# A convolution block on one core: reordered seams between stages, and products that nothing reads

## The chip, the cores and the metric

The kernel runs on one core of one Trainium2 chip. Its measure is the device time of one execution in microseconds (us); where several executions are timed, their median counts. A separate execution was recorded by the hardware profiler. All operands are 32-bit floats.

## The reference

The input x has 16 images of 192 channels and 64 x 64 pixels. The first layer computes

```python
h = ln2d(x)                                    # over the channels of each pixel
projected, gate = split(conv1x1(h, 192 -> 384))
projected = dwconv3(projected, dw_k)
scanned = mix of four directional scans of projected (lr, rl, tb, bt)
mixed = (scanned + dwconv3(projected, le_k)) * sigmoid(gate)
mixed = gelu(batch_norm(mixed))                # mean and variance over all images and pixels
x = x + conv1x1(mixed, out_proj)
x = x + conv1x1(gelu(conv1x1(ln2d(x), fc1: 192 -> 768)), fc2: 768 -> 192)
```

The second layer averages every image over its pixels, passes the averages through two small matrices (192 to 48 to 192 x 9) and so gets a 3 x 3 filter for each channel of each image, of which a mask keeps four taps. It filters each image with its own taps and adds a bias.

## The kernel before

The work is in three stages, each with its own pools in SBUF. The order of instructions on every engine is written out by hand; nothing is planned by the framework. Images go in pairs, one on partitions 0 to 63 and one on 64 to 127; `HALF` names these two slices, and the 192 channels are three tiles of 64, indexed by `t`.

**First stage** (lines 246 to 584): 64 chunks of four pixel groups (`AR`). `load_a` (L466) fetches a chunk three chunks ahead, one image from SP and one from GpSimd. `turn` (L479) transposes a chunk on TensorE (L484) into the one PSUM tile `xt`, so that VectorE can take the statistics of each pixel (`variance`, L488: L491 and L492). `deviation` (L494) gets the reciprocal root with ScalarE (L496) and VectorE (L497). `project` (L500) multiplies the untransposed pixels with the projection weights (L512), two PSUM tiles for each image half, and evicts with the scale of each pixel, on VectorE (L517) and ScalarE (L518), into a staging tile: `stg` for even blocks of four chunks, `mid` for odd ones. `store` (L533) writes a block to DRAM during the next four chunks, on GpSimd and SP, so a staging tile has to be stored before the block after the next writes it. Ahead of the loop, `projection_weights` (L272) scales the weights on VectorE (L277), takes their column means on TensorE (L281) and subtracts them (L284). Small jobs hang on chunk numbers by `beside`: among them `load_dm` and `load_lm` (L186, L192), which fetch the second stage's filter matrices, half from SP and half from GpSimd.

**Second stage** (lines 587 to 789): 24 groups of eight channels, 96 steps. Vertical and local filters are products with banded matrices (L618, L662), horizontal scans run on VectorE (L653, L655), `gate` (L686) multiplies by the sigmoid and, at the end of a group, stores it to `mixed_d` in DRAM (L704). The statistics of the batch norm end with `spread` (L715) and `batch_norm` (L726). The last group lies in `mid`.

**Third stage** (lines 792 to 1096): 128 chunks of 512 pixel positions. `load_y` (L209) fetches two chunks of `mixed_d`, for the first eight chunks into `ximg[1]`, which is not used yet; `unmix` (L844) transposes them back on VectorE (L239), `bn_gelu` (L850) is on ScalarE (L852, L853), `out_proj` (L874: L880 for channels 128 to 191, L884 for 0 to 127) on TensorE, `residual` (L887) adds the input `x2` into the image tile `ximg` (L890) and forms the sums over channel tiles (L894, L905). `mean` (L907, L913) turns such sums into means; `center` (L915, L920) subtracts them, `squares` (L924) squares (L927) and sums again (L928, L905), `normalize` (L933) takes the root (L936), loads the Gelu table by a one-element activation (L938), and multiplies by the reciprocal (L939, L940). `first` (L942) is the product with fc1 (L952) and its GELU (L954), `second` (L957) that with fc2 (L825, called from `both`), `final` (L966) adds it to the image (L972). The loop at L1057 interleaves one step of each of several chunks, from -3 on:

```python
    for n in range(-3, n_ch + 1):
        at(load, n + 3)
        at(unmix, early_)
        at(first, n, 0)
        at(bn_gelu, early_)
        products(n, 0)
```

`products(n, t)` (L855) puts a mean of chunk n + 1 and the output product of chunk n + 2 into one PSUM tile of two banks, tag `f1`, of which there are two and which `first` uses too. Tag `f2` has three banks, tag `a` one. When a pair's last chunk is final, `pooled`, `squeeze` (L988) and `excite` (its products again are L825, tile `ps_k`) give the taps.

**The tail** (lines 1098 to 1118) filters the last pair in 12 pieces of 16 rows (four row groups by three channel tiles): five on ScalarE (L1026) and VectorE (L65), seven as products with taps on diagonals (L1103, L1035) evicted by ScalarE (L1037). All use an output tile `ol` of tag `gl`, of which there are four. The pieces are stored from SP, GpSimd and ScalarE (L1041, L1044).

## Time and profile before

| | |
|---|---|
| median of 3 runs | 3750.83 us (3748.33 to 3751.44) |
| profiled execution, its own time | 3738.29 us |
| its span, first to last instruction | 3736.5 us |
| TensorE busy | 3686.8 us, 99% of the span |
| VectorE busy | 2706.0 us, 72% |
| ScalarE busy | 1786.6 us, 48% |
| GpSimd busy | 420.2 us, 11% |
| mean granted clock of TensorE | 0.994 |

In the profile PE is TensorE's matrix product, PEld its weight load, DVE VectorE, ACT ScalarE, POOL GpSimd and SP the engine that only issues transfers; POOLq, ACTq and SPq are their queues. A line such as "L952 PE MATMUL ps_f<-h,wf" gives the line of the kernel, the engine, the operation, and the tile written and read. A 32-bit product appears as two records, a transpose as one. "Granted clock" is the share of TensorE's full clock that it was allowed. Times in the timeline count from the start of the span. The first stage takes the time up to about 636 us, the second to about 1310, the third the rest, the tail its last 40.

### The profile page before, as it was taken

The page shows a single profiled execution, that of the slowest core. Times are in us where ns is not written, and L with a number is a line of the kernel's source. Part 1 is how long each engine was busy: PE and PEld are TensorE (multiplying, and loading weights), DVE is VectorE, ACT ScalarE, POOL GpSimd, SP SyncE. Part 2 cuts the span into 40 slices and gives each one's busy share as a digit, 9 for nine tenths or more (in the row PEclk, how much of TensorE's full clock was granted, in tenths as well). Part 3 has the DMA queues.
Part 4 walks back from the last instruction along what each step waited for, and adds up shares of the span by engine and source line. Part 5 has one row for each costly group of instructions (what it writes and reads, how often), then busy time and mean ns, then how long its engine had stood idle before and what let it go on. Part 6 is the DMA issues. An engine that isn't in the chain of part 4 may idle for free.

```text
span 3736.5 us, 71017 instructions
## 1 busy us (share of the span) xinstructions
PE 3686.8 (99%) x30252; PEld 1649.4 (44%) x30252; DVE 2706.0 (72%) x4164; ACT 1786.6 (48%) x1945; POOL 420.2 (11%) x683
## 2 busy tenths in 40 slices
PE   8999999999999979999999999999999999999998
PEld 5666656555555533333333333333333333333333
DVE  6887776999999965557666766766766766675763
ACT  3434434888888833334334434434443443443432
POOL 2334332101011020000000000000000000000000
PEclk9999999999999989999999999999999999999999
DMA  6899997999999841112212222222222221221212
GB/s 163 241 252 243 265 280 238 308 294 283 280 283 271 226 100 27 51 44 63 78 56 66 69 67 62 69 61 68 74 57 58 76 71 42 80 75 43 69 37 74
DMA packets 308427, 491.74 MB, mean 132 GB/s; under 512 B 46656, under 2 KB 202640, under 8 KB 308112
## 3 DMA queue, kind: packets, MB, share of 16 engines
q1 hardware_dynamic: 250064, 295.14, 29.5%
q0 software_dynamic: 57152, 190.94, 18.7%
q8 instruction: 239, 3.92, 0.4%
q10 hardware_dynamic: 896, 1.12, 0.1%
q14 instruction: 76, 0.62, 0.1%
HBM read 284.91 MB, written 197.92 MB: 129 GB/s over the span
## 4 chain that ended last, share of the span: by engine, by line
PE 96%; DMA 2%; DVE 1%; SPq 0%; POOL 0%; issue 0%; ACT 0%; ACTq 0%; DVEq 0%; POOLq 0%
PE ps_f L952 27%; PE ps_f L825 27%; PE ps_pj L512 12%; PE ps_l L662 11%; PE ps_d L618 7%; PE ps_o L884 5%; PE ps_xt L484 2%; PE ps_o L880 2%; PE ps_o L913 1%; DMA xa<-in_x_dram 1%; PE ps_k L825 0%; DMA ximg<-mixed_d 0%; DMA mixed_d<-mid 0%; SPq L472 0%; PE ps_d L1035 0%
## 5 line engine op out<-in xcount | busy, mean ns | idle before, releaser
L954 ACT ACTIVATE gl<-ps_f,bf 128x1024 f32<-128x1024 f32 x384 | 427.6, 1114 | 1316.2 <-PE ps_f L952 1316.2
L952 PE MATMUL ps_f<-h,wf 64*64 64x512 f32 x9216 | 1035.8, 594 | 6.8 <-DVE h L940 6.7
L825 PE MATMUL ps_f<-gl,place 128*64 128x512 f32 x4608 | 1022.2, 592 | 0.0
L952 PEld LDWEIGHTS ps_f<-h,wf 64*64 64x64 f32 x9216 | 334.5, 133 | 693.8 <-issue 642.6
L825 PEld LDWEIGHTS ps_f<-gl,place 128*64 128x64 f32 x4608 | 334.2, 137 | 574.5 <-issue 533.4
L512 PE MATMUL ps_pj<-wi,xa 64*128 64x384 f32 x3072 | 515.6, 488 | 3.5 <-DVE stg L517 3.5
L920 DVE TENSOR_TENSOR h<-ximg,ps_o 128x768 f32<-128x768 f32 x128 | 116.4, 951 | 425.3 <-PE ps_o L884 417.0
L512 PEld LDWEIGHTS ps_pj<-wi,xa 64*128 64x128 f32 x3072 | 294.3, 187 | 196.8 <-issue 12.2
L890 DVE SCALAR_TENSOR_TENSOR ximg<-ps_o,pt,low 128x256 f32<-128x256 f32 x384 | 168.0, 479 | 266.8 <-PE ps_o L884 266.8
L65 DVE SCALAR_TENSOR_TENSOR o<-ximg,taps,o 128x1024 f32<-128x1024 f32 x252 | 323.2, 1282 | 9.1 <-ACT o L1011 2.6
L1015 POOL DMA_DIRECT2D out_dram<-o x168 | 87.9, 528 | 2067.6 <-DVE o L65 2064.8
L939 DVE RECIPROCAL rs<-rs 128x512 f32<-128x512 f32 x64 | 214.3, 3349 | 27.0 <-ACT rs L936 27.0
L653 DVE TENSOR_TENSOR_SCAN v<-tab,q 128x1024 f32<-128x1024 f32 x96 | 218.3, 2274 | 6.8 <-ACT tab L641 6.8
L655 DVE TENSOR_TENSOR_SCAN v<-tab,q 128x1024 f32<-128x1024 f32 x96 | 217.5, 2266 | 0.0
L518 ACT ACTIVATE stg<-ps_pj,rsa 128x384 f32<-128x384 f32 x128 | 120.5, 945 | 188.7 <-PE ps_pj L512 178.5
L884 PE MATMUL ps_o<-low,wo 128*64 128x256 f32 x1536 | 210.0, 395 | 0.0
L641 ACT ACTIVATE tab<-mask,dec_b 128x1024 f32<-128x1024 f32 x192 | 209.8, 1146 | 0.0
L518 ACT ACTIVATE mid<-ps_pj,rsa 128x384 f32<-128x384 f32 x128 | 120.8, 944 | 181.7 <-PE ps_pj L512 174.7
L491 DVE BATCH_NORM_STATS2 st<-ps_xt 128x6 f32<-128x192 f32 x512 | 173.8, 340 | 17.3 <-PE ps_xt L484 17.1
L239 DVE STREAM_TRANSPOSE low<-low 128x512 f32<-128x512 f32 x174 | 167.7, 1016 | 2.1 <-issue 0.3
L972 DVE SCALAR_TENSOR_TENSOR ximg<-ps_f,pt,ximg 128x512 f32<-128x512 f32 x192 | 134.4, 749 | 40.2 <-PE ps_f L825 37.8
L472 POOL DMA_DIRECT2D xa<-in_x_dram x192 | 119.8, 630 | 362.6 <-PE ps_pj L512 285.0
(197 smaller groups left out, 4060.1 us busy)
## 6 DMA issues: line engine op xcount, KB each, us to landing
low<-in_x_dram SPq DMA_DIRECT2D x128, 384.0 KB
out_dram<-o POOLq DMA_DIRECT2D x168, 256.0 KB, 3.7
mid<-pg_d SPq DMA_DIRECT2D x8, 4096.0 KB
low<-mixed_d SPq DMA_DIRECT2D x116, 256.0 KB
low<-pg_d SPq DMA_DIRECT2D x7, 4096.0 KB
pg_o<-pg_d SPq DMA_DIRECT2D x7, 4096.0 KB
xa<-in_x_dram POOLq DMA_DIRECT2D x192, 128.0 KB, 5.6
xa<-in_x_dram SPq DMA_DIRECT2D x192, 128.0 KB
```

Source lines behind the costliest of these rows:

```text
L65: nc.vector.scalar_tensor_tensor(o, in0, scalar, in1, ALU.mult, ALU.add, **kw)
L512: nc.tensor.matmul(ps[i], pixels(n, t, g)[q], wi[q, t].rearrange("p g k c -> p (g k c)"), start=(t == 0), stop=(t == 2))
L518: nc.scalar.activation(stag[blk][1][:, :, j], ps[1], AF.Copy, scale=rs[:, g, 1:2])
L618: nc.tensor.matmul(dst(ps[o, ih]), mats[g % 2]["dm"][q, di + 1, :, ch], src(s["pg"][q, :, 0, ch]), start=(di == 0), stop=stop)
L653: nc.vector.tensor_tensor_scan(vf, tab, q, 0.0, ALU.mult, ALU.add)
L655: nc.vector.tensor_tensor_scan(vf[:, ::-1], tab[:, ::-1], q[:, ::-1], 0.0, ALU.mult, ALU.add)
L662: nc.tensor.matmul(dst(bst[k]["ps"][o, i]), lm_of(g)[q, m, :, c], src(q, ih), start=start, stop=stop)
L825: nc.tensor.matmul(ps[q], w(i), rhs(i), start=start, stop=stop)
L884: nc.tensor.matmul(ps[q, wh].rearrange("p (r w) -> p r w", w=32), wo[:, 64 * t:64 * t + 64], cols(rows(s["mx"][:, i]))[:, :, wh], start=Fa ...
L939: nc.vector.reciprocal(rs, rs)
L952: nc.tensor.matmul(pf[o, i], wf1[q, t, m0:m0 + 64], s["h"][q, t], start=(t == 0), stop=(t == 2))
L954: nc.scalar.activation(gl, pf, AF.Gelu, bias=bf1[:, m:m + 1])
```

## The change

It has six parts.

1. Opening: `ones` is set first, and 24 products of `ones` with `ones` follow on TensorE, which nothing reads. The weights' means and their subtraction stand ahead of the first transposes. In chunk 0, the first two pixel groups are projected ahead of chunk 1's transposes, and chunk 1's statistics are taken beside the last two groups, two groups' worth beside each.
2. The four loads of filter matrices hang on chunks 46, 48, 50 and 52 instead of 46 to 49.
3. `mid` is the first tile of its pool, and `ximg[1]` is allocated ahead of `ximg[0]`, so `ximg[1]` and not `ximg[0]` lies where `mid` was.
4. The store of the last group is cut in two, half from SP and half from GpSimd.
5. The loop of the third stage starts at chunk 1. What came before is written out: chunk 0's output product takes the columns of channels 0 to 127 first, the means of chunk 0 come from products over all three channel tiles (`mean_part`) instead of from sums on VectorE, they lie in a bank of their own, the squares are taken in two halves, the Sqrt table is loaded early, and the output products of chunks 0 to 2 are placed between. `idle(k)` issues k products that nothing reads, of 128 x 128 weights and 512 columns: two before the output product of chunk 0, one ahead of `first(0, 0)`; in the last chunk two behind `pooled` and one behind `excite`.
6. The tail's five pieces on ScalarE and VectorE write to tiles of tags `o` and `h2`.

```diff
+    mid = ce.tile([128, SB_], F32, tag="mid", name="mid")
     ones = ce.tile([128, 128], F32, tag="ones", name="ones")
...
-        beside(46, load_dm, 0)
-        beside(47, load_lm, 0)
-        beside(48, load_dm, 1)
-        beside(49, load_lm, 1)
+        for i in range(2):
+            beside(46 + 4 * i, load_dm, i)
+            beside(48 + 4 * i, load_lm, i)
...
-        def project(n):
+        def project(n, groups, beside_it):
...
-            for g in range(AR):
+            for g in groups:
...
-                if n + 1 < n_ac:
-                    variance(n + 1, g)
+                for v in beside_it(g) if n + 1 < n_ac else ():
+                    variance(n + 1, v)
...
+        nc.vector.memset(ones, 1.0)
+
+        idle = bank()
+        for _ in range(24):
+            nc.tensor.matmul(idle[:, 0:128], ones, ones, start=True, stop=True)
         make_identity(nc, ident)
...
         decays()
+        next(steps)
+        next(steps)
         turn(0)
-        next(steps)
         for g in range(AR):
             variance(0, g)
-        next(steps)
         deviation(0)
...
+            h = AR // 2 if n == 0 else 0
+            project(n, range(h), lambda g: ())
             if n + 1 < n_ac:
                 turn(n + 1)
-            project(n)
+            project(n, range(h, AR), lambda g: (g,) if h == 0 else (2 * (g - h), 2 * (g - h) + 1))
...
-                nc.gpsimd.dma_start(mixed_d[:, :, :, g].rearrange("i b p e -> p (i b) e"),
-                                    s["pg"][:, :, 0].rearrange("p n c j -> p n (c j)"))
+                parts = ((nc.gpsimd, 0, n_half),) if g < NCG - 1 else ((nc.sync, 0, n_half // 2), (nc.gpsimd, n_half // 2, n_half))
+                for queue, i0, i1 in parts:
+                    queue.dma_start(mixed_d[i0:i1, :, :, g].rearrange("i b p e -> p (i b) e"),
+                                    s["pg"][:, i0 * NB:i1 * NB, 0].rearrange("p n c j -> p n (c j)"))
...
-    ximg = [k3.tile([128, 3, HW + 1, RW], F32, tag=f"ximg{i}", name=f"ximg{i}") for i in range(n_img)]
+    ximg = [k3.tile([128, 3, HW + 1, RW], F32, tag=f"ximg{i}", name=f"ximg{i}") for i in (1, 0)][::-1]
...
     def out_proj(n, t, ps):
+        if n == 0:
+            out_columns(n, t, ps, True)
+            out_quarters(n, t, ps, False)
+        else:
+            out_quarters(n, t, ps, True)
+            out_columns(n, t, ps, False)
...
+        if n == 0:
+            return
         if t == 1:
             s["sum"] = hp2.tile([128, 3, HCH], F32, tag="sm", name="sm", bufs=1)
...
+    def mean_part(n, pm, t, k, src):
+        for i, q in enumerate(HALF):
+            nc.tensor.matmul(pm[q, k], mean64[q], src[q], start=(t == 0 and k == 0), stop=(t == 2 and k == 1))
...
-        o = wp.tile([128, GR, HW], F32, tag="gl", name="ol", bufs=4)
+        if dg is None:
+            o = (op.tile([128, GR, HW], F32, tag="o", name="o") if g < 2 else
+                 hp2.tile([128, 3, CH], F32, tag="h2", name="ol")[:, 0:2].rearrange("p k (h w) -> p (k h) w", w=HW))
+        else:
+            o = wp.tile([128, GR, HW], F32, tag="gl", name="ol", bufs=4)
...
+    def out_alone(n, t, later=False):
+        if later:
+            ps = [ps2.tile([128, CH], F32, tag="f2", name="ps_o2", bufs=3)[:, 0:HCH] for _ in range(2)]
+        else:
+            pair = ps2.tile([128, 2, CH], F32, tag="f1", name="ps_o", bufs=2)
+            ps = [pair[:, wh, 0:HCH] for wh in range(2)]
+        out_proj(n, t, ps)
+        if not later:
+            residual(n, t, ps)
+        return ps
+
+    def one_bank():
+        return ps2.tile([128, 2, HCH], F32, tag="a", name="ps_m")
+
+    def idle(k):
+        ps = ps2.tile([128, CH], F32, tag="a", name="ps_i")
+        for _ in range(k):
+            nc.tensor.matmul(ps, ident, wf1[:, 0, 0:CH], start=True, stop=True)
+
+    idle(2)
+    load_y(2, ys[1], (nc.sync, nc.gpsimd))
+    border(ximg[0])
+    for n in range(2):
+        load(n)
+        unmix(n)
+        bn_gelu(n)
...
+    for t in range(3):
+        out_alone(0, t)
+        if t:
+            for k in range(2):
+                mean_part(0, pm, t - 1, k, img0[:, t - 1, halves[k]])
+    for k in range(2):
+        mean_part(0, pm, 2, k, img0[:, 2, halves[k]])
+    center(0, pm)
+    load(2)
...
+        nc.scalar.activation(sq0[:, k], st[0]["h"].rearrange("p t (k n) -> p k t n", k=2)[:, k], AF.Square)
+    nc.scalar.activation(warm, eps6, AF.Sqrt)
+    out_alone(1, 0)
+    pw = one_bank()
+    for k in range(2):
+        for t in range(3):
+            mean_part(0, pw, t, k, sq0[:, k, t])
+    st[0]["pw"] = pw
+    normalize(0)
+    load_y(4, ys[2], (nc.gpsimd,))
+    residual(1, 1, out_alone(1, 1, True))
+    out_alone(1, 2)
+    idle(1)
+    first(0, 0)
+    pm = ps2.tile([128, 2, CH], F32, tag="f1", name="ps_o", bufs=2)[:, :, 0:HCH]
+    mean(1, pm, "sm")
+    unmix(2)
+    center(1, pm)
+    bn_gelu(2)
+    squares(1)
+    load(3)
+    first(0, 1)
+    unmix(3)
+    out_alone(2, 0)
+    second(0, 0)
+    bn_gelu(3)
+    products(0, 1)
+    normalize(1)
+    first(0, 2)
+    products(0, 2)
+    second(0, 1)
+    nc.vector.memset(pool2, 0.0)
+
+    for n in range(1, n_ch + 1):
...
             pooled(ended)
+            if ended == n_pairs - 1:
+                idle(2)
...
             excite(ended)
+            if ended == n_pairs - 1:
+                idle(1)
```

## The prediction

> **What bounds the kernel now.** I read the page's slices first (TensorE at 99% busy, its granted clock lower in few places), then the list of what TensorE waited for, then the timeline around each wait. Of its idle time the releasers are these (columns: engine and line, released by, us in total, times, longest):
>
> ```profile
> PE ps_xt L484 <- DMA xa<-in_x_dram: 11.8, 4, 9.3
> PE ps_f L952 <- DVE h L940: 6.7, 1, 6.7
> PE ps_o L913 <- DVE sq L905: 4.8, 1, 4.8
> PE pm L720 <- DVE stats L694: 4.6, 1, 4.6
> PE ps_o L880 <- ACT low L853: 3.8, 1, 3.8
> PE ps_pj L512 <- DVE stg L517: 3.5, 2, 3.0
> ```
>
> Everything that TensorE lacks sits at the opening, at the turn from the second to the third stage, at one place in the first stage (the last row) and at the end. Elsewhere it runs without a gap, so nothing is won there. Idle time also lowers the clock. Windows of the second seam (TensorE, its loads, VectorE, ScalarE, GpSimd busy; then the granted clock, DMA share, GB/s):
>
> ```profile
> 1330.00:1332.00 2.00, 0.00 (x0) 0.00 (x0) 2.00 (x3) 0.11 (x1) 2.00 (x4) 1.00 0.87 243
> 1332.00:1334.00 2.00, 0.00 (x0) 0.00 (x0) 1.16 (x3) 1.37 (x1) 2.00 (x4) 0.69 1.20 197
> 1334.00:1336.00 2.00, 1.30 (x9) 0.90 (x10) 1.78 (x5) 0.00 (x0) 0.78 (x2) 0.50 0.90 133
> 1352.00:1354.00 2.00, 2.00 (x16) 0.60 (x12) 2.00 (x4) 1.37 (x2) 0.00 (x0) 0.69 1.14 142
> ```
>
> The clock is halved some 2.8 us after the last product (1329.9) and comes back 5.3 us after the first of L952 (1348.1). In the same way it fell 2.5 us after 1306.4 and 5.0 us after 1341.4, and rose 4.1 us after 1318.2.
>
> **Part 1, the opening.** The timeline:
>
> ```profile
> 13.60 1.09 PE L484 MATMUL ps_xt<-ident,xa 128*128 128x128 f32 x4 [0.79 <-DMA xa<-in_x_dram]
> 14.61 4.21 PE L281 MATMUL pb<-wi,wf 64*128 64x384 f32 x6
> 18.75 2.82 PE L484 MATMUL ps_xt<-ident,xa 128*128 128x128 f32 x12
> ```
>
> The 12 transposes at 18.75 take 2.82 us against 1.53 later: all is cold up to some 22. The change adds 24 products before the first work, puts L281 and L284 ahead of the first transposes, and chunk 0's first two pixel groups ahead of chunk 1's transposes.
>
> One product of 128x128 is two records. Cold, L720 (half as many columns) took 1.08 us for four; warm, a 128-column transpose takes 0.13. So 48 records: 6 us if all were warm, 18 if all cold at 0.38. With some 5 us cold I take 11, so they end at 12. Here a rule speaks against the change: the Trainium skill, "TensorE: Matmul & The Clock Gate" (Part 3, The mechanism), has matmuls in strict first-in first-out order, so fillers push real work back. The weights are ready at 9.2 (L277), so 12 costs 2.8 us of that: L281 warm (2.1) to 14.1, transposes to 15.6. L284 (1.5), the eight statistics pairs (3.9) and the root (0.4) end at 19.9 on VectorE. Groups 0 and 1 run meanwhile, 15.6 to 19.6; evictions, chunk 1's statistics (twice as many per group) and evictions end so that chunk 1's transposes and statistics release chunk 2's transposes at 26.4, done 27.9. Now they are done at 31.2: 3.3 us saved. Fillers ended by 9.3: 4.5. Ended at 14.6: 0.6. The input transfers are issued as before, and the last of chunk 0 lands at 13.5, before TensorE needs it.
>
> **Part 2, the filter matrices.** At 482 chunk 48 waits for its staging buffer, whose last store SP issued at 480.14 behind the first matrix load (1.94 us on SP at 474.85), taking some 7.4 us to land. TensorE idles 3.0 us, then runs 24 records in 5.83 instead of 4.04 us: 5.0 lost in all. Each pair of matrices is 1.44 MB by its tiles' shapes, over 5 us of transfers that are already 0.9 to 1.05 busy. The change leaves the first load at chunk 46, so SP's delay stays; the second goes to 48, past that boundary, on both SP and POOL. That frees GpSimd's half (327 KB, 1.3 us): the stall falls to 1.7 and is too short for the cold tail. But the third load, now at 50, stands before the next boundary's store in the same way. Ends: nothing (a second stall like it) and 5.0 (both hidden). I take 2.5, their middle.
>
> **Part 3, the second seam.** The lines that set it:
>
> ```profile
> 1321.80 0.88 DVE L890 SCALAR_TENSOR_TENSOR ximg<-ps_o,pt,low 128x256 f32<-128x256 f32 x2 [2.02 <-PE ps_o L884]
> 1329.96 1.82 DVE L920 TENSOR_TENSOR h<-ximg,ps_o 128x768 f32<-128x768 f32 x2 [2.19 <-PE ps_o L884]
> 1340.78 1.28 ACT L936 ACT_TABLE_LOAD   x1 [7.41 <-DVE ximg L890]
> 1342.79 3.35 DVE L939 RECIPROCAL rs<-rs 128x512 f32<-128x512 f32 x1 [1.36 <-ACT rs L936]
> 1348.09 7.91 PE L952 MATMUL ps_f<-h,wf 64*64 64x512 f32 x48 [6.71 <-DVE h L940]
> ```
>
> Centring (L920) and the root (L936) each wait for work of chunk 1 that shares their PSUM tile. New times:
> - The first output product starts with the columns that need only the first GELU, ready at 1317.4, not 1318.2. The two fillers (two records of 512 columns over the whole array, each as long as two of L825's 0.215 us: 0.86 us warm, 1.7 cold) run from 1314.4 to 1317.8, so it starts at 1317.8 and the clock is back near 1318.5.
> - Residuals of chunk 0 are no longer held by the last mixed_d store: L890 began at 1321.80 when the store landed at 1321.71, TensorE having been done 0.6 us before. With `mid` allocated first, ximg[0] doesn't lie on it. They end at 1324.3 (1326.0 now).
> - The sums (L894, L905: 2.46 us) give way to 12 means products, of which 4 come after the last residual, 0.5 us. Centring 1325.0 to 1326.8: 5.0 earlier.
> - Two half squares on ScalarE, 12 means products in a bank of their own, Sqrt's table loaded early. Root at 1329.2 instead of 1342.07: it follows the end of centring by 2.4 instead of 10.3, 7.9 more.
> - Root, reciprocal (3.35) and multiply (1.76) as now: first(0,0) at 1335.2, 12.9 earlier.
>
> Then TensorE has 3 x 5.3 (first), 2 x 5.15 (second), three output products at 1.44 and a mean: 31.4 us; two short waits for PSUM (0.7 and 0.4 us) make 32.4. first(1,0) follows at 1367.6; now 1383.06. The sum is 15.5. Sixteen extra means products (some 1.7 us) lie in TensorE's waits. VectorE has 24.5 us of work in those 32.4; without that slack it would be the next one late. unmix(2) needs the y load, whose SP and POOL halves are issued behind the store and then 3 us to landing each: about 1330, wanted at 1339. load(2), on SP behind it, needs to land by 1351. The borders and load_y(4) keep their order on GpSimd; load_y(4) took 11 to 12 us to land and is wanted after 1366, where its cover ends.
>
> A hole of 2.9 us (1332.3 to 1335.2) remains. The trace's clock fell after 2.5, 2.8 and 5.0 us; the Trainium skill, "TensorE: Matmul & The Clock Gate" (What's actually happening), has one idle window of 3.4. By the page nothing is lost, by the trace's shorter rows the 2.6 us that the cold L952 lost (7.91 against 5.31): 15.5 or 12.9. I take 15.5; ends 11 and 17.
>
> The split store: 10.77 us to land. The Trainium skill, "Trainium Kernel Development and Optimization" (Key Constraints), says that a second issuing engine saves only issue time, here half of GpSimd's 1.75; the slow ramp of the DMA share (0.14, 0.37, then 1.0) allows 3. Neither counts, as y is not on this path.
>
> **Part 4, the tail.**
>
> ```profile
> 3698.48 2.72 PE L825 MATMUL ps_k<-red,w2t 48*64 48x1 f32 x48 [0.62 <-DVE red L991]
> 3701.95 15.52 PE L1035 MATMUL ps_d<-ximg,low 64*64 64x512 f32 x128 [0.75 <-PE ps_k L825]
> 3730.58 1.11 ACT L1037 ACTIVATE ol<-ps_d,pt 128x1024 f32<-128x1024 f32 x1 [2.75 <-DMA out_dram<-ol]
> ```
>
> Two fillers (1.7 us from 3696.0) delay the squeeze by 0.3, but L825 should run warm, half of 2.72, and the first 64 records of L1035 lose their 1.5 us of cold. So L1035 starts at 3700.9 and its 7 pieces of 32 records (3.5 us at L952's 0.11) end at 3725.4 instead of 3729.0. ScalarE's waits for an output buffer (11.0 us, the last 2.75 at the very end) go, as five pieces get buffers elsewhere; last eviction 3726.6 instead of 3731.7. The output is 6.3 MB: at the present mean of 237 GB/s from 3707 it ends at 3733.3 (2 saved), at the 300 that its mean DMA share of 0.79 leaves room for, TensorE sets the end (5.1). I take 5.0; ends 2 and 6.5.
>
> **Sum.** 3.3 + 2.5 + 15.5 + 5.0 = 26.3. The profiled execution's own time is 3738.3 (span 3736.5), which gives 3712.0. The median is 3750.8, 12.5 above it; I carry the same gap over: 3724.5.
>
> **Rivals.**
> - The clock: products of constants don't hold it. Then the opening gains 1 at most, the seam 12.9, the tail 2.5, with 2.5 for part 2: 19, so 3732. For it: the transposes ran 2.75 us cold after seven busy ones, and after the 48 one-column records of `ps_k` the clock was still halved. Against it: with L952 and L880 any dense run brought it back within 5.3 us, and the fillers are denser. Chance 0.16.
> - Transfers: the third matrix load stalls a second boundary (part 2 worth 0) and output bandwidth ends the run (tail 2): 20.8, so 3730. For it: DMA shares near 1.0 at both places. Chance 0.22.
> - Slower: the y load. unmix(2) stands in VectorE's queue ahead of centring chunk 1, so TensorE starves behind one late load. Landing after 1339.3 pushes the seam one for one; from 1339.3 + 26.3 = 1365.6 the kernel is slower, at 1376 it is 3761. Against it: these loads land in 3 us. Chance 0.03.
> - The rest (some of the gains cancelled by waits that I don't see): no change, 0.02.
>
> **How the numbers follow.** My forecast has 0.57, its own range 3719 to 3729. The other two fast cases are inside 3715 to 3737, whose top is the bad ends of all parts added (0.6 + 0 + 11 + 2 = 13.6, so 3737) and whose bottom leaves room for the good ends (33, so 3718) and the spread of the three runs. This measurement can tell about 0.2%, 7.5 us. Faster 0.95, same 0.02, slower 0.03.
>
> **What would show it.** L281 in some 2 us and chunk 2's transposes done near 28; no 3 us gap at the boundary near 480; first(0,0) some 13 us and first(1,0) some 15 us earlier relative to the last gate; L825 `ps_k` near 1.4 us, no DMA releaser ahead of ScalarE's last evictions. I'm wrong if y's transposes wait for a DMA, if the clock row still shows halves at the seam, or if a new wait shows in chunks 1 to 3 of the third stage.

## The result, and the profile after

The changed kernel takes 3723.51 us (median, 3721.87 to 3724.84) where the kernel before takes 3749.58 us in the same set of runs. The ratio is 0.9931, with a 95% interval of 0.9914 to 0.9948: 26 us faster, between 19.5 and 32. The forecast was 3724.5.

The profiled execution has a span of 3720.1 us, its own time 3721.87, a mean clock of 0.996. Against the profile of before, that is only 16.4 us. The reason is the kernel before: its timed executions range from 3738.8 to 3761.1 us over all sets of runs, and the profiled one (3738.29) was faster than any of them. So below, each stretch is compared over several profiles where there are any, and each total over many runs. The list of what TensorE waits for, after:

```profile
PE pm L729 <- DVE stats L701: 4.6, 1, 4.6
PE ps_pj L512 <- DVE stg L517: 2.9, 1, 2.9
PE ps_xt L483 <- DMA xa<-in_x_dram: 2.5, 2, 2.0
PE ps_f L981 <- DVE h L969: 1.8, 1, 1.8
```

The waits of the second seam have gone from the top: L952's 6.7 us for `h` is now 1.8 (line L981), and L913's and L880's are no longer listed. The opening's 9.3 us wait for `xa` is gone, since fillers and the weights' means (L281) now stand ahead of it. One wait did not change, that of L729 for the batch statistics. One in the first stage, L512 for `stg`, was in the list of before too, but here it lies at another place: chunk 32 and not chunk 48.

The opening, in the timeline of after:

```profile
1.05 8.37 PE L548 MATMUL pb<-ones 128*128 128x128 f32 x48 [1.05 <-DVE ones L544]
9.48 2.20 PE L281 MATMUL pb<-wi,wf 64*128 64x384 f32 x6
14.68 0.63 PE L483 MATMUL ps_xt<-ident,xa 128*128 128x128 f32 x4 [1.97 <-DMA xa<-in_x_dram]
15.23 4.14 PE L512 MATMUL ps_pj<-wi,xa 64*128 64x384 f32 x24
25.73 1.50 PE L483 MATMUL ps_xt<-ident,xa 128*128 128x128 f32 x12 [0.74 <-PE ps_pj L512]
```

The 24 fillers end at 9.42, and L281 runs warm behind them (2.20 us; 4.21 before). The trace's record of the granted clock begins with its first rise, at 22.04 us before and at 6.85 after; up to there the profile's clock row reads 1.00, and only the durations tell. The transposes wait 1.97 us for the last piece of chunk 0. Chunk 2's transposes (the last row) end at 27.2, where before they ended at 31.2.

The second seam, in the timeline of after (its last gate, L699, starts at 1305.29; that of before at 1308.31):

```profile
1311.59 3.78 PE L1109 MATMUL ps_i<-wf,ident 128*128 128x512 f32 x4 [0.25 <-DVE mv L742]
1315.30 1.98 PE L906 MATMUL ps_o<-low,wo 128*64 128x256 f32 x8
...
1324.23 1.82 DVE L949 TENSOR_TENSOR h<-ximg,ps_m 128x768 f32<-128x768 f32 x2 [1.19 <-PE ps_m L942]
1329.04 0.69 ACT L965 ACTIVATE rs<-ps_m,eps 128x512 f32<-128x512 f32 x1 [0.60 <-PE ps_m L942]
1329.76 3.35 DVE L968 RECIPROCAL rs<-rs 128x512 f32<-128x512 f32 x1 [2.92 <-ACT rs L965]
1334.96 5.38 PE L981 MATMUL ps_f<-h,wf 64*64 64x512 f32 x48 [1.85 <-DVE h L969]
```

Centring (L949) and root (L965) are now released by TensorE's means, with waits of 1.19 and 0.60 us. `first(0, 0)` starts 29.67 us behind the gate (39.78 before) and takes 5.38 us instead of 7.91. `first(1, 0)` starts 62.69 behind the gate (74.68 before); its rows, before and after:

```profile
1382.99 5.38 PE L952 MATMUL ps_f<-h,wf 64*64 64x512 f32 x48
```

```profile
1367.98 5.38 PE L981 MATMUL ps_f<-h,wf 64*64 64x512 f32 x48
```

Windows of the seam in after (columns as in the prediction):

```profile
1315.00:1317.00 2.00, 2.00 (x9) 0.77 (x8) 1.79 (x2) 1.23 (x2) 0.00 (x0) 0.50 0.75 223
1317.00:1319.00 2.00, 2.00 (x22) 0.83 (x20) 0.88 (x2) 0.84 (x2) 1.07 (x3) 0.86 0.20 49
1333.00:1335.00 2.00, 0.15 (x5) 0.04 (x4) 1.97 (x3) 0.00 (x0) 0.00 (x0) 1.00 1.06 137
```

The clock is still 0.50 under the first output product, as under the fillers ahead of it, and it comes back at some 1317.6. From then on it stays at 1.00, past the hole ahead of L981.

The tail, in the timeline of after:

```profile
3683.99 1.56 PE L835 MATMUL ps_k<-red,w2t 48*64 48x1 f32 x48 [0.62 <-DVE red L1020]
3685.82 1.53 PE L1109 MATMUL ps_i<-wf,ident 128*128 128x512 f32 x2 [0.27 <-DVE taps L1030]
3687.28 25.51 PE L1068 MATMUL ps_d<-ximg,low 64*64 64x512 f32 x224
3714.22 1.11 ACT L1070 ACTIVATE ol<-ps_d,pt 128x1024 f32<-128x1024 f32 x1 [3.67 <-DMA out_dram<-o]
```

`ps_k` takes 1.56 us instead of 2.72, but L1068 then stands behind a filler of 1.53 us. The last eviction still waits for a transfer, 3.67 us, of which 1.4 lie behind the end of TensorE's last product.

### The profile page after: what moved, and what is told of

Its sections match the earlier page's. It is cut to its first block, busy times and chain, and to the rows that moved or that the text cites. A ratio compares the mean times of both kernels' runs of the same rounds, so it can differ in the third digit from the quotient of the medians.

```text
span 3720.1 us, 71189 instructions
## 1 busy us (share of the span) xinstructions
PE 3694.2 (99%) x30344; PEld 1644.7 (44%) x30344; DVE 2699.1 (73%) x4154; ACT 1785.3 (48%) x1947; POOL 419.6 (11%) x683
## 3 DMA queue, kind: packets, MB, share of 16 engines
q0 software_dynamic: 56896, 189.89, 18.9%
## 4 chain that ended last, share of the span: by engine, by line
PE 98%; DVE 1%; DMA 1%; ACT 0%; issue 0%; SPq 0%; POOL 0%; ACTq 0%
PE ps_f L981 27%; PE ps_f L835 27%; PE ps_pj L512 14%; PE ps_l L669 11%; PE ps_d L625 7%; PE ps_o L906 5%; PE ps_xt L483 2%; PE ps_o L899 2%; PE ps_o L937 1%; DMA xa<-in_x_dram 0%; PE ps_k L835 0%; PE ps_d L1068 0%; PE ps_i L1109 0%; DVE v L662 0%; DVE v L660 0%; DMA pg_d<-mid 0%
## 5 line engine op out<-in xcount | busy, mean ns | idle before, releaser
L981 PE MATMUL ps_f<-h,wf 64*64 64x512 f32 x9216 | 1033.3, 593 | 3.0 <-DVE h L969 1.8
L835 PE MATMUL ps_f<-gl,place 128*64 128x512 f32 x4608 | 1022.2, 592 | 0.0
L981 PEld LDWEIGHTS ps_f<-h,wf 64*64 64x64 f32 x9216 | 333.6, 133 | 688.4 <-issue 633.7
L835 PEld LDWEIGHTS ps_f<-gl,place 128*64 128x64 f32 x4608 | 334.2, 137 | 574.5 <-issue 533.4
L512 PE MATMUL ps_pj<-wi,xa 64*128 64x384 f32 x3072 | 515.4, 488 | 2.9 <-DVE stg L517 2.9
L949 DVE TENSOR_TENSOR h<-ximg,ps_o 128x768 f32<-128x768 f32 x126 | 114.5, 950 | 420.9 <-PE ps_o L906 412.6
L512 PEld LDWEIGHTS ps_pj<-wi,xa 64*128 64x128 f32 x3072 | 294.4, 187 | 195.4 <-issue 12.2
L65 DVE SCALAR_TENSOR_TENSOR o<-ximg,taps,o 128x1024 f32<-128x1024 f32 x261 | 334.7, 1282 | 9.3 <-ACT o L1040 2.6
```

What stands on the lines that cost most here:

```text
L65: nc.vector.scalar_tensor_tensor(o, in0, scalar, in1, ALU.mult, ALU.add, **kw)
L512: nc.tensor.matmul(ps[i], pixels(n, t, g)[q], wi[q, t].rearrange("p g k c -> p (g k c)"), start=(t == 0), stop=(t == 2))
L835: nc.tensor.matmul(ps[q], w(i), rhs(i), start=start, stop=stop)
L981: nc.tensor.matmul(pf[o, i], wf1[q, t, m0:m0 + 64], s["h"][q, t], start=(t == 0), stop=(t == 2))
```

## The experiments

The kernel before had a median of 3747 us in the first two sets of runs and 3750.4 in the third (the last four experiments), so ratios to it are compared. The changed kernel's is 0.9931 (0.9914 to 0.9948), and every run that alters one part of it has an interval that overlaps this one. So the times alone settle only what the filter matrices are worth (respaced_only); what any other part is worth is read from positions in the traces, mostly in one profile each. Behind each heading stands the edit. Positions are counted from the start of the last gate (seam) or from the end of the last L835 of chunk tile `ps_f` (tail).

**again** is the kernel before, unchanged, profiled once more.

> The kernel before, profiled once more. Its first profile lay 11 us under the median of its timed runs (3738.3 against 3749.6), the changed kernel's only 1.6 under (3721.9 against 3723.5). Theory of the staging waits: in most executions of the kernel before, TensorE loses some 5 us at one or more further block boundaries of the first stage, where a staging buffer's last store lands late; then this profile, if it lands near 3750, shows two or three gaps of about 3 us released by DVE stg L517 or DVE mid L517 instead of one, and the rest of the timeline as in the first. Rival: the lost time is spread over all stages (a few tenths per chunk); then no extra gap shows, and the stages' lengths grow in proportion.

Measured: 3746.74 us, ratio 1.0 (0.9992 to 1.0008). In its profile (own time 3755.91) the list of TensorE's waits has, where the first profile had 3.5 us:

```profile
PE ps_pj L512 <- DVE stg L517: 11.9, 2, 10.1
```

The 10.1 us are at chunk 32, where the first profile had 0.4. Seam and tail: `first(1, 0)` at 75.66 (74.68 in the first profile), tail 42.9 (40.5). So much of the difference between two single profiles is one stall of the first stage, which comes and goes in both kernels: in the profile of after it was 2.9 us, followed by 24 cold records (5.84 us instead of 4.14). The theory of staging waits held, with one long stall in place of two or three of 3 us. The first profile of before is the odd one: in the eleven other profiles whose small stores stand where they did, the wait at chunk 32 is 2.9 to 11.2 us.

**respaced_only** takes the kernel before and does part 2 alone.

```diff
-        beside(46, load_dm, 0)
-        beside(47, load_lm, 0)
-        beside(48, load_dm, 1)
-        beside(49, load_lm, 1)
+        for i in range(2):
+            beside(46 + 4 * i, load_dm, i)
+            beside(48 + 4 * i, load_lm, i)
```

> The kernel before with only the four filter-matrix loads moved to chunks 46, 48, 50, 52. Theory of the staging waits: the 3 us gap at chunk 48 and the cold 24 records behind it (5.0 us in all) go, no gap takes their place at chunk 52, median 3744 to 3745. My own sum had 2.5 (3747). Rival: the third load stalls chunk 52 instead, median 3749 to 3750.

Measured: 3744.71 us, ratio 0.9989 (0.9983 to 0.9996), 1.5 to 6.4 us faster. The gap at chunk 48 is 1.35 us with no cold stretch behind it (3.0 and some 2 us of cold before), and there is none at chunk 52.

**respacing_undone** takes the changed kernel and puts the loads back on chunks 46 to 49.

> The changed kernel with the filter-matrix loads back at chunks 46, 47, 48, 49. Theory of the staging waits: a gap of about 3 us at chunk 48 comes back, median 3728.5. My sum: 3726. Rival (the respacing does nothing in the changed order): 3723.5.

Measured: 3725.27 us, ratio 0.9945 (0.9931 to 0.9958). TensorE's waits for `stg` (the longer one is at chunk 32), and then the one at chunk 48 in the timeline:

```profile
PE ps_pj L513 <- DVE stg L518: 5.2, 2, 3.1
```

```profile
476.04 2.16 SPq L190 DMA_DIRECT2D dm<-dv_d  x1
481.16 1.40 SPq L537 DMA_DIRECT2D pg_d<-stg  x2
489.75 2.93 PE L513 MATMUL ps_pj<-wi,xa 64*128 64x384 f32 x8 [2.09 <-DVE stg L518]
```

The stall is back at the old place. The first matrix load (L190) ahead of the block's last store (L537) is not enough for it: in after it stands there too (1.59 us at 473.20, the last store at 478.74), and chunk 48 does not wait. What the edit puts back is the second load beside it, on GpSimd at 476.01 and on SP at 482.60. In the three profiles with the loads on chunks 46 to 49 the wait at chunk 48 is 1.87 to 3.04 us, in the eleven with the loads spaced out it is 0 to 1.35. By the ratios part 2 is worth 4.1 us in respaced_only (1.5 to 6.4) and 5.2 here, where the two intervals overlap.

**no_opening_fillers** leaves out the 24 products of `ones` and keeps the new order.

```diff
-        idle = bank()
-        for _ in range(24):
-            nc.tensor.matmul(idle[:, 0:128], ones, ones, start=True, stop=True)
```

> The changed kernel without the 24 products of ones at the opening, the reordering kept. If the fillers hold the clock: L281 takes 4.2 us again instead of 2.2 and the first two pixel groups run cold (8 us instead of 4.1), so chunk 2's transposes end near 29.5 instead of 27.2, median 3725 to 3726. Rival (the order alone brings the gain): 27.2 and 3723.5.

Measured: 3724.51 us, ratio 0.9940 (0.9927 to 0.9952). Timeline:

```profile
8.79 4.21 PE L281 MATMUL pb<-wi,wf 64*128 64x384 f32 x6 [8.79 <-DVE wi L277]
12.93 2.82 PE L483 MATMUL ps_xt<-ident,xa 128*128 128x128 f32 x12
27.74 4.46 PE L512 MATMUL ps_pj<-wi,xa 64*128 64x384 f32 x26
```

All is cold up to some 16 us (the clock first rises at 16.27), yet chunk 1's products start at 27.74, against 27.16 in after and 31.15 before the change. So the order brings most of the gain. What the fillers add is not shown: over the ten profiles that have them, chunk 1's products start anywhere from 25.1 to 29.1 us. In after the transposes wait for the last piece of x, which lands at some 14.7 us. In five of the ten the clock, once raised, falls again between 10.8 and 16.1 us, and chunk 1's products start at 28.1 us in the mean of these five, at 26.3 in that of the others.

**no_seam_fillers** leaves out `idle(2)` and `idle(1)` of the second seam.

> The changed kernel without the fillers of the second seam: neither the two before chunk 0's output product nor the one ahead of first(0,0). If they hold the clock: the clock comes back about 1 us later in the output products of chunk 0, and the hole of some 3 us ahead of first(0,0) halves it again, so that first(0,0) takes up to 7.9 us instead of 5.4; from the last gate to first(1,0) 64 to 66 us instead of 62.8. If they are idle work: 62.8 or, since two cold fillers stand in front of the first output product (0.9 us), 62.

Measured: 3726.22 us, ratio 0.9943 (0.9936 to 0.9951). Its last gate starts at 1325.25. Two rows of the timeline:

```profile
1334.43 1.98 PE L906 MATMUL ps_o<-low,wo 128*64 128x256 f32 x8 [3.13 <-ACT low L862]
1355.77 5.38 PE L981 MATMUL ps_f<-h,wf 64*64 64x512 f32 x48 [3.00 <-DVE h L969]
```

The output product starts 0.8 us earlier, since no filler stands ahead of it, but the clock comes back 14.9 us behind the gate instead of 12.3, so `first(0, 0)` starts at 30.52, 0.85 later than in after, and `first(1, 0)` at 63.52, short of the 64 to 66 expected. In the other profiles with this order `first(0, 0)` starts at 28.9 to 29.7, so the delay stands out, though from one profile. The hole of 3.00 us ahead of L981 does not lower the clock here.

**tail_buffers_undone** puts the tail's five pieces back into the four tiles of tag `gl`.

> The changed kernel with all twelve pieces of the tail on the four gl buffers again. My prediction (the buffers free 3.6 us and more): from the end of the last L825 of the last chunk to the end of the span 42.5 us or more instead of 39.1. Rival (the output's transfers set the end, whatever buffer they leave from): 39 to 40.

Measured: 3725.01 us, ratio 0.9945 (0.9929 to 0.9961); tail 40.7 us against 38.0 to 39.2 in the seven profiles that keep the tail as it is; it lies between the two expectations. ScalarE's waits for a transfer are back in the middle of the tail, and TensorE ends at 32.19 instead of 31.82. By this profile the buffers are worth some 2 us, more than half of what the tail gained; the three profiles of the old tail spread over 40.5 to 42.9, so the rest is not apportioned.

**no_tail_fillers** leaves out `idle(2)` behind `pooled` and `idle(1)` behind `excite`.

> The changed kernel without the two fillers behind pooled and the one behind excite. My prediction (they hold the clock into the taps' products): 2.7 us lost, 41.8 instead of 39.1 from the last L825 to the end. What the changed kernel's trace suggests: the excite products cost 1.2 more, but the squeeze comes 0.5 earlier and the filler behind excite (1.53 us, itself cold) is out of the way; L1068 starts 6.0 us behind the last L825 as against 6.3, runs cold either way, and the end is the same within 0.5.

Measured: 3722.41 us, ratio 0.9938 (0.9916 to 0.9961); tail 38.9. Timeline:

```profile
3684.22 2.72 PE L835 MATMUL ps_k<-red,w2t 48*64 48x1 f32 x48 [0.62 <-DVE red L1020]
3687.70 25.74 PE L1068 MATMUL ps_d<-ximg,low 64*64 64x512 f32 x224 [0.75 <-PE ps_k L835]
```

`ps_k` is cold again, but nothing stands between it and L1068, which starts 5.98 us behind the last L835 (6.31 with fillers) and ends 31.71 behind it (31.82). In this profile the fillers of the tail are worth nothing.

**allocation_undone** gives `mid` and `ximg` their old places (part 3 undone; the lines below are those for `ximg`) and keeps the split store.

```diff
-    ximg = [k3.tile([128, 3, HW + 1, RW], F32, tag=f"ximg{i}", name=f"ximg{i}") for i in (1, 0)][::-1]
+    ximg = [k3.tile([128, 3, HW + 1, RW], F32, tag=f"ximg{i}", name=f"ximg{i}") for i in range(n_img)]
```

> The changed kernel with mid at its old place and ximg[0] first again, so that ximg[0] lies on mid. My prediction (residuals held by the store of the last group): the first residual starts only when that store has landed, some 9.5 us after it is issued at two queues, about 12 us behind the last gate, not before; it starts 12.8 us behind the gate in the changed kernel, so at two queues the wait just vanishes and 0 to 0.5 us is lost. With the store slower than that (10.8 as before) 1 us. Rival (nothing was held there even before): 0, and no transfer named as releaser.

Measured: 3724.81 us, ratio 0.9945 (0.9920 to 0.9969). The first residual starts at 12.78 (12.81 in the changed kernel). Nothing is won by the places once the store is cut in two: the y loads that wait for it start at 1319.06, so it has landed before TensorE's first products end (1319.67), and nothing was left to hold. With the store in one piece, as before, the places were not tried.

**stores_spread** goes after the stall that both kernels share. SP and GpSimd issue the small stores to `lv_d` (L416, pieces of 16 bytes), and loads of `xa` behind one of them stay on SP for 13.19 us at 305.89 in the profile of after. The edit hangs them on other chunks.

```diff
+        spread = {3: (18, 20, 21, 22), 4: (25, 26, 28, 29), 5: (32, 33, 34, 36), 6: (37, 38, 40, 41), 7: (42, 44, 45, 46)}
...
-                beside(end + 1 + part, store_vector, k, part)
+                beside(spread[k][part] if k > 2 else end + 1 + part, store_vector, k, part)
```

> The changed kernel, with the small stores of the first stage (lv_d, L416, in pieces of 16 bytes) hung on chunks 18 to 46, one to a chunk, and none on the two chunks ahead of chunk 32 or on the last chunk of a block. Theory that these stores delay the staging block's last store: the wait of L512 for stg at chunk 32 (2.9 us in the profile of the changed kernel, 0.4 to 11.2 in the other profiles, with a cold stretch behind the long ones) falls to at most 1 us, and no new one of more than 1 us appears; the median falls by 3 to 8 us against the changed kernel, to about 3718, and its runs lie closer together. Rival, that the store is late for another reason or that the delay only moves to chunk 36, 40 or 44: the sum of these waits stays, median 3722 to 3725.

Measured: 3734.22 us, ratio 0.9954 (0.9940 to 0.9968): probably slower than the changed kernel, whose interval it just overlaps, and not faster as expected. TensorE's waits, and the place in the timeline:

```profile
PE ps_pj L513 <- DVE mid L518: 5.8, 1, 5.8
PE ps_xt L484 <- DMA xa<-in_x_dram: 4.5, 2, 2.9
```

```profile
434.99 1.23 SPq L416 DMA_DIRECT2D lv_d<-gt  x1
439.25 6.39 SPq L472 DMA_DIRECT2D xa<-in_x_dram  x3
445.68 1.28 SPq L537 DMA_DIRECT2D pg_d<-mid  x2
454.82 1.64 PE L513 MATMUL ps_pj<-wi,xa 64*128 64x384 f32 x2 [5.77 <-DVE mid L518]
```

Chunk 32 is free of it, and the stall stands at chunk 44 instead, longer. The rival that the delay only moves was right, except that the waits grew (5.8 and 1.4 us at chunk 44). That the stall moved with the stores speaks for them as its cause; but on chunks 40 to 44 they meet the weight loads of the later stages, so how much each adds stays open.

**stores_spread_fewer_fillers** is the same without the fillers of the tail and the one ahead of `first(0, 0)`.

> The run before with the fillers taken out that earlier runs put at nothing: the one ahead of first(0, 0) and all three at the end. Theory that they are worth nothing: the same within 1 us as with them; ps_k takes 2.7 us instead of 1.6 but ps_d starts no later behind the last L835. Rival, that they hold the clock: first(0, 0) takes 7.9 us instead of 5.4, and the tail is 2 us longer; 4 us slower in all.

Measured: 3736.25 us, ratio 0.9958 (0.9943 to 0.9972). The hole ahead of `first(0, 0)` is as long as in no_seam_fillers, but here the clock falls. `first(0, 0)`:

```profile
1351.77 6.76 PE L982 MATMUL ps_f<-h,wf 64*64 64x512 f32 x48 [2.99 <-DVE h L970]
```

The product takes 1.4 us longer. So this filler is worth something in some executions and nothing in others; the expectation that it was worth nothing was wrong. In the tail, too, one profile does not settle it: without fillers `ps_k` took 1.66 us here, as if warm, but the clock fell right behind it, TensorE ended at 32.05 and the tail was 39.9 us, against 38.8 in the mean of the seven profiles with fillers.

**root_shares_tile** puts one thing of the old seam back: the means of the squares lie in one tile with half of the output product (1, 1), whose residual stands ahead of the root.

```diff
-    pw = one_bank()
+    pair = ps2.tile([128, 2, CH], F32, tag="f1", name="ps_o", bufs=2)
+    pw = pair[:, 0].rearrange("p (k n) -> p k n", k=2)
+    po = [pair[:, 1, 0:HCH], ps2.tile([128, CH], F32, tag="f2", name="ps_o2", bufs=3)[:, 0:HCH]]
...
+    out_proj(1, 1, po)
+    residual(1, 1, po)
     normalize(0)
     load_y(4, ys[2], (nc.gpsimd,))
-    residual(1, 1, out_alone(1, 1, True))
```

> The changed kernel, with one part of the seam put back in the old form: the means of chunk 0's squares lie in one PSUM tile (not in one bank) with half of the output product (1, 1), and the residual of that product stands ahead of the root, as before. Theory that whoever reads a tile waits for the others that read it: the root (L965) starts behind that residual, some 26.0 us behind the last gate instead of 23.75, released by VectorE; first(0, 0) starts 32.0 us behind the gate instead of 29.7 and first(1, 0) at 65.0 instead of 62.7, or at 67.5 if TensorE's longer hole of some 5 us halves the clock. Rival, that a shared tile costs nothing where the banks differ: the root still starts at 23.75, released by TensorE, though the reciprocal behind it then stands behind the residual on VectorE, so that first(0, 0) is at 32.0 here too. The kernel's time: 2 to 5 us longer than the changed kernel's.

Measured: 3730.04 us, ratio 0.9940 (0.9924 to 0.9956), in the third set. Its last gate starts at 1309.95. Timeline:

```profile
1334.43 0.92 DVE L912 SCALAR_TENSOR_TENSOR ximg<-ps_o,pt,low 128x256 f32<-128x256 f32 x2 [3.21 <-PE ps_o L906]
1334.95 0.69 ACT L965 ACTIVATE rs<-ps_o,eps 128x512 f32<-128x512 f32 x1 [2.12 <-DVE ximg L912]
1341.27 7.08 PE L981 MATMUL ps_f<-h,wf 64*64 64x512 f32 x48 [3.80 <-DVE h L969]
```

The root is released by VectorE's read of the other bank of its tile, 25.0 us behind the gate. `first(0, 0)` starts at 31.32 and, the hole being 3.80 us, runs cold for a while (7.08 us). `first(1, 0)` starts at 66.03, 3.3 later than in the changed kernel; the timed ratio alone does not show it. The mechanism that the prediction read out of the old seam is shown for the root. It is worth 1.2 us of the root's start, where 2.2 were expected; the rest of the root's gain (33.8 to 23.75 behind the gate: the means by products, the squares in halves, the early table) and the own bank for the means of chunk 0 were not put back by any run, and rest on the timelines.

**late_stores_left_out** does not write the last three pieces that ScalarE and VectorE compute.

> The changed kernel without the stores of the last three pieces of the tail that ScalarE and VectorE compute (L1074, row groups 2 and 3 of channels 0 to 63, row group 0 of channels 64 to 127): 1.6 MB of the output are not written. Theory that the output transfers set the end: the last eviction (L1070) no longer waits 3.7 us for a buffer and starts behind TensorE, and the tail, from the end of the last L835 of f2 to the end, falls from 39.1 to 36.0 us or less. Rival, that TensorE and its eviction set the end: it falls by 1.4 us at the most, to 37.7 or more.

Measured: 3727.72 us, ratio 0.9938 (0.9919 to 0.9958); tail 37.7 us. The last eviction:

```profile
3720.62 1.11 ACT L1070 ACTIVATE ol<-ps_d,pt 128x1024 f32<-128x1024 f32 x1 [2.32 <-DMA out_dram<-ol]
```

It starts 0.08 us behind TensorE's last product (3720.54) and 5.8 us before the end. With a quarter of the output's bytes gone the tail is about 1 us shorter, which is no more than the last eviction's wait for a buffer behind TensorE (1.4 us in after). So TensorE's end, the eviction and one store's issue and landing set the end; the output's transfers cost that wait for a buffer at the most.

## Why the prediction was right

The sum was right, and most of its mechanisms; two of its four terms were too large, by 2.8 and 1.7 us, and the other two probably too small. That the forecast came within 1 us is in part luck, the more so as the runs give the gain only to within 6 us. Seam and tail are compared as means: three profiles of before's seam and tail (before, again, respaced_only) against those of after and of the experiments that leave the stretch as it is (seven each), the opening as the mean of the same three and of the ten with fillers.

| part | predicted | measured | from |
|---|---|---|---|
| opening | 3.3 | 3.7 | chunk 1's products, 30.9 to 27.2 |
| filter matrices | 2.5 | 4.1 (1.5 to 6.4) | respaced_only |
| second seam | 15.5 | 12.7 | `first(1, 0)` behind the gate, 75.1 to 62.4 |
| tail | 5.0 | 3.3 | end of last L835 to the end, 42.1 to 38.8 |
| sum | 26.3 | 23.8 | the runs: 26.1 (19.5 to 32.2) |

The two first profiles differ by less. Read off the starts of the same instructions, after gains 4.0 in the opening, loses 5.0 at chunk 32 (2.86 of wait for 0.41, the cold stretch, smaller shifts), gains 5.6 from chunk 48 to the end of the first stage, loses 1.6 at the start of the second, and gains 12.0 in the seam and 1.4 in the tail: 16.4. The prediction added the 12.5 us between the profile of before and its median to the new sum. The changed kernel's own profile lies 1.6 us under its median, so that gap was no property of a profiled execution: it stood, at least in good part, for stalls such as chunk 32's, which the first profile of before happened to miss. Medians have them on both sides, so the forecast came out right against the median, as it would not have against the profile.

**The opening.** The fillers' size was a wrong term: 48 records take 8.37 us, 0.17 each, not 11. Its basis, four records in 1.08 us, does not carry over to a long row, where a microsecond takes in six or seven records while cold and eleven from 7 us on. The fillers end at 9.42, when the weights are ready, so the 2.8 us that the first-in first-out rule of the Trainium skill ("TensorE: Matmul & The Clock Gate", Part 3, The mechanism) would cost did not arise. The other wrong term balanced it: "the last of chunk 0 lands at 13.5, before TensorE needs it". It landed at 14.7 and TensorE waited 1.97 us.

**The filter matrices.** The mechanism was right: the second load freed the boundary, with a stall of 1.7 predicted and 1.35 measured in respaced_only (0 in after), no cold stretch behind it and no second stall at chunk 52. The fear of that second stall had halved the term, which came out nearer to 4 than to 2.5.

**The seam.** Counted from the gate, the prediction had residuals end at 16.0, centring at 16.7, root at 20.9, `first(0, 0)` at 26.9 and `first(1, 0)` at 59.3. Measured: 17.8, 18.9, 23.75, 29.67 and 62.69. Half of the 3.4 us are lost before the residuals end: the output product starts at 10.0 instead of 9.5, and the clock is back at 12.3 instead of 10.2, so most of the first output product runs cold. The fillers take 3.78 us, not 3.4, but above all the clock did not come back within the time assumed: 6.0 us behind their start, where 4.1 had been carried over from the old seam (4.3 by the changes of the clock in the trace: 1318.18 to 1322.52). In the other profiles with these fillers it comes back 10.5 to 12.3 us behind the gate, so 10.2 was earlier than any. Root and centring add 1.1 us between them. The claim on the residuals, that the place of `ximg[0]` held them, is neither shown nor refuted: the old places cost nothing with the store cut in two (allocation_undone), which lands in time either way. At most it was 0.6 us, the time from TensorE's end to L890 in the old seam. Of the two steps that carry the part, the root freed of chunk 1's residual is shown (root_shares_tile), the own bank for the means of chunk 0 fits the timeline: centring now waits for these means alone.

**The hole ahead of `first(0, 0)`.** Page and trace had been weighed at 15.5 against 12.9, and nothing was lost in the changed kernel. But there are three other holes by now: 3.00 us without a drop (no_seam_fillers), 2.99 us with one (stores_spread_fewer_fillers, 1.4 us lost), and 3.80 us with one although a filler stands ahead of it (root_shares_tile, 1.7 us lost). No fixed length decides. The clock of the traces shows what does: in each of the 14 profiles all changes of the granted clock lie whole multiples of 3.413 us apart, as if it were set anew once in each such stretch. The stretches around the hole, first in stores_spread_fewer_fillers, then in no_seam_fillers (columns as before):

```profile
1347.78:1351.19 3.41, 0.99 (x8) 0.39 (x8) 3.38 (x2) 0.18 (x1) 0.00 (x0) 1.00 0.94 167
1351.19:1354.60 3.41, 2.83 (x16) 1.14 (x20) 3.31 (x8) 0.00 (x0) 0.00 (x0) 0.50 0.99 92
```

```profile
1350.35:1353.76 3.41, 2.42 (x24) 0.97 (x20) 3.29 (x1) 1.57 (x3) 0.00 (x0) 1.00 1.00 174
1353.76:1357.17 3.41, 1.41 (x16) 0.70 (x20) 3.34 (x6) 0.00 (x0) 0.00 (x0) 1.00 1.06 99
```

In the first the hole lies in one stretch and leaves 0.99 us of work in it, and the clock falls at its end. In the second a boundary cuts the hole, 2.42 and 1.41 us of work are left, and the clock stays. So the filler ahead of `first(0, 0)` buys safety against the phase, which differs between the executions here. The Trainium skill ("TensorE: Matmul & The Clock Gate", What's actually happening) says that the window of activity is free-running, so that the point of a transition moves between executions; these rows agree with that. Its idle window of some 3.4 us fits in length, but the window need not be idle throughout: the one that ends in the drop has 0.99 us of work.

**The tail.** The failing step is "L1035 starts at 3700.9", 1.05 us earlier than before. It starts 0.33 later (6.31 behind the last L835 for 5.98), since the third filler stands in its way, and it still starts cold. TensorE therefore ends 1.25 us earlier and not 3.6: that is the buffers' doing, as TensorE no longer waits for ScalarE (25.5 us for the seven pieces instead of 27.1). "ScalarE's waits for an output buffer go" held in after for all but the last, which still costs 1.4 us.

**The rivals.** Clock: products of constants do raise the clock, in the opening (first rise at 6.85 us with them, at 16.27 without) and in the seam (back 12.3 us behind the gate with them, 14.9 without), though what that is worth in the opening is not shown. In the tail they don't hold it over `ps_k` and the third filler. Transfers: the third matrix load stalls nothing, and the output's transfers cost at most the last eviction's wait. The y load was not late: `unmix(2)` ran at 1339.05 behind VectorE's own work, with no wait for a transfer.

## What to carry to other kernels

Give a short chain its own PSUM tile and put the work of the next chunk behind it in the order: the reordered seam made half of the gain, while fillers were worth at most about a microsecond where that could be read off, and nothing clear of the spread where the next product has to queue behind them. Before you sum up terms against one profile, profile the kernel before a second time: a stall that varies by 10 us between executions is larger than most terms. Moving stores of tiny pieces away from a stall moved the stall along with them here.

## What the runs showed of the hardware

- The granted clock changes on a grid of 3.413 us whose phase differs from one execution to the next (14 profiles, 85 falls). It fell behind stretches in which products of more than 8 columns filled at most 0.41 of the time, with one exception (0.65), and it rose only behind stretches that they filled to at least 0.83. So it came back 2.8 us behind the first product in stores_spread_fewer_fillers and 6.0 us behind the first filler in the seam of after.
- Products of one column keep TensorE "busy" without holding its clock. At the start of the second stage of after, 36 records of one column (L140) fill the whole stretch; the clock falls at its end and stays at 0.50 until 641.73. In before it falls in the same way at 639.85 but is back at 643.27, and with the longer cold time the start took 1.6 us more in after. In the tail of after the clock falls at 3686.42, behind the 48 records of `ps_k`.

```profile
631.49:634.90 3.41, 3.41 (x32) 3.41 (x33) 0.00 (x0) 0.00 (x0) 3.13 (x6) 1.00 0.58 130
634.90:638.31 3.41, 3.41 (x20) 1.79 (x23) 0.16 (x1) 0.00 (x0) 0.00 (x0) 0.50 0.96 305
```

- Loads can stay on their queue long behind a store in pieces of 16 bytes: at the same place in the first stage three loads of `xa` took 9.84 us (before), 13.19 (after), 13.78 (no_seam_fillers) and 16.73 (again). In after, three such loads take 2 to 9 us at the other places, behind other stores of this kind too, so the size of the pieces alone does not make the delay.
